# A selective-scan layer in double steps, with a column for the first state ahead of each scan

## The chip, the core and the metric

The kernel runs on one core of one Trainium2 chip. The metric is the device time of one execution in microseconds (us). The engines are TensorE (PE in the profile, PEld for its weight loads), VectorE (DVE), ScalarE (ACT), GpSimd (POOL) and SyncE (SP), which issues the DMAs. SBUF is the on-chip working memory, PSUM the memory that TensorE writes to.

## What is computed

Four layers stand one behind the other on an image batch of 3 x 256 channels x 48 x 48, each as x + layer(groupnorm(x)): a convolution block with attention, a convolution with weights mixed from eight experts, a plain 3x3 convolution, and a selective state space layer (Mamba). Only the last one is touched by the change. It is, for tokens l of one image:

```
xn = layernorm(x)                         # over the 256 channels
x_in, z = in_proj(xn)                     # 512 channels each
u = silu(causal_conv(x_in))               # 4 taps
dt_raw, B, C = x_proj(u)                  # 16 + 16 + 16 values a token
dt = softplus(dt_proj(dt_raw) + bias)
h[d, n] = h[d, n] * exp(dt[d] * A[d, n]) + dt[d] * u[d] * B[n]     # token by token, 16 states n
y[d] = sum over n of h[d, n] * C[n] + u[d] * D[d]
out = out_proj(y * silu(z)),  x = x + out
```

## The kernel before

The layer's code starts at L995. The 2304 tokens of an image are cut into chunks of CH = 384, six an image, 18 in all. The 512 inner channels are four blocks m of 128. For the recurrence the partitions hold 32 channels times 4 states: a block m has four quarters q of 32 channels, and the 16 states are four groups g of four. So one chunk has 4 (m) x 4 (g) = 16 steps of 4 scans (q), and one scan is one VectorE instruction over 128 partitions and 384 tokens.

The main loop (L1348) goes over `steps`, 288 of them. Step s does:

- `fill(s + 1)`: the inputs dt*u*B of the next step's scans, into a tile `hs`. VectorE makes the first two quarters (L1291) from `ps_r`, rows that TensorE has spread over the partitions (`spread_pe`, L1273); GpSimd makes the other two (L1292) from rows that DMAs have spread (`spread`).
- four scans (L1360) in place on `hs`. Each multiplies by a decay exp(dt*A), which ScalarE has written to a PSUM tile `ps_da` (`decay`, L1304), and starts from a state of the chunk before (`state[m, g]`, a per-partition operand), or from 0.0 in the first chunk of an image. The decays come from a pool of three tiles, and behind the scan with running number n the decay n + 3 is issued.
- a ScalarE copy of the last column of the four scans to `state[m, g]` (L1372).
- the product with C on GpSimd (L1375) into a tile `hc`.
- `add_states(s - 2)`: TensorE sums the states of one channel (L1320) into `ps_y`, which also gets u*D (L1316).
- `gate`, two steps into the next block: VectorE multiplies `ps_y` by silu(z) (L1327).

Beside this the loop does the work for the chunks around the present one. `plan`, `after` and `gating` list stages by place: the number j = 4m + g of the step, and where in it (MID: behind the second scan; LATE: behind the fourth; PE_: behind add_states). The stages share one PSUM tile of two banks, `bank` (`ps_g`). Those of interest here: `group_scale` (ScalarE, L1062), `channel_mean` (TensorE, L1069), `centre` (VectorE subtraction L1075, ScalarE square L1077), `inverse_root` (ScalarE, L1081), `normalise` (VectorE, L1086), `tokens` (ScalarE, L1096), `taps` (TensorE, L1105), `take_u` (ScalarE, L1112), `silu` (ScalarE with a table load before and after, L1117), `softplus` (ScalarE, three instructions, L1157), `take_dt` (VectorE twice, L1163, then a ScalarE copy), `project_y` (TensorE, L1188) and `store` (VectorE addition of the residual, L1199, then the DMA out).

`keep_order` (L1397) ties PE, DVE, ACT and POOL to the order in which the source issues. So each of these engines works through its list in that order, and an instruction that waits holds up all that stand behind it on its engine. Which instruction waits for which count of which engine's semaphore is worked out by the tile framework from the tiles that are read and written. SP's list is not tied.

Of the kernel before, what the change touches and what calls it, by code (L numbers as in the profile page):

```python
# [9 lines left out]
F32 = mybir.dt.float32  # L10
I32 = mybir.dt.int32
AF = mybir.ActivationFunctionType
ALU = mybir.AluOpType
AX = mybir.AxisListType
PSUM = bass.MemoryType.PSUM

P = 128
# [3 lines left out]
CT = 2  # L21
# [4 lines left out]
CH = 384  # L26
NCH = N // CH
# [7 lines left out]
DI = 4  # L35
# [47 lines left out]
def net(  # L83
# [20 lines left out]
    nc = tc.nc  # L104
# [13 lines left out]
    def v(name, i=0, n=1):  # L118
# [3 lines left out]
    ident = const.tile([P, P], F32, name="ident")  # L122
# [6 lines left out]
        out=gview, in_=gview, pattern=[[-8, 16], [0, 8]], compare_op=ALU.is_ge,  # L129
# [3 lines left out]
        out=gview, in_=gview, pattern=[[8, 16], [0, 8]], compare_op=ALU.is_ge,  # L133
# [4 lines left out]
    mean2 = const.tile([P, P], F32, name="mean2")  # L138
# [205 lines left out]
    with ExitStack() as l0:  # L344
# [39 lines left out]
        with ExitStack() as p1:  # L384
# [3 lines left out]
            for b in ORDER:  # L388
# [12 lines left out]
                for m in range(2):  # L401
                    for ct in range(CT):
                        nc.tensor.matmul(
                            pb[:, m : m + 1], w("cv1", ct * 256 + m * P, P), sh[:, ct : ct + 1],
                            start=ct == 0, stop=ct == CT - 1,
                        )
                bb = small.tile([P, 2], F32, name="bb")
# [3 lines left out]
                for c in range(NCH):  # L411
                    for m, dst in ((0, y1), (1, cur[b])):
                        pm = ps.tile([P, 512], F32, tag="s", name="ps_y")
                        for ct in range(CT):
                            nc.tensor.matmul(
                                pm[:, :CH], ws[:, ct, m * P : (m + 1) * P], chunk(xb[:, ct, :], c),
                                start=ct == 0, stop=ct == CT - 1,
# [67 lines left out]
        with ExitStack() as p2:  # L485
# [9 lines left out]
            for i in range(NB):  # L495
# [268 lines left out]
                for mt in range(0, NT, 2):  # L764
                    pv = pair()
                    for j in range(2):
                        nc.tensor.matmul(
                            pv[:, j, :384], cur[2][:, (mt + j) * P : (mt + j + 1) * P], wn[2],
                            start=True, stop=True,
# [19 lines left out]
                if i + 1 < NB:  # L789
# [4 lines left out]
                    for b in ORDER:  # L794
                        for c in range(NCH):
                            f = hidden(b, c)
# [69 lines left out]
        chunks = [(b, c) for b in ORDER for c in range(NCH)]  # L866
# [15 lines left out]
        for n, b in enumerate(ORDER):  # L882
            held = None
            for c in range(NCH):
                f = hidden(b, c)
# [31 lines left out]
    with ExitStack() as l1:  # L917
# [55 lines left out]
        for n, (k, h) in enumerate(halves):  # L973
            layer, b = units[k]
# [17 lines left out]

    with ExitStack() as l3:  # L995
        wp = l3.enter_context(tc.tile_pool(name="w3", bufs=1))
        act = l3.enter_context(tc.tile_pool(name="act", bufs=2))
        scn = l3.enter_context(tc.tile_pool(name="scn", bufs=2))
        psd = l3.enter_context(tc.tile_pool(name="psd", bufs=3, space=PSUM))
        psr = l3.enter_context(tc.tile_pool(name="psr", bufs=1, space=PSUM))  # L1000
        psg = l3.enter_context(tc.tile_pool(name="psg", bufs=1, space=PSUM))
        psy = l3.enter_context(tc.tile_pool(name="psy", bufs=1, space=PSUM))
# [32 lines left out]
            )  # L1035
        fold = rep[:, 0, :]

        diag = wp.tile([P, DI, P], F32, name="diag")
        for m in range(DI):
            nc.vector.tensor_scalar(diag[:, m, :], ident, v("D", m), None, ALU.mult)  # L1040
# [3 lines left out]
        def fetch(at):  # L1044
            k = chunks[at] = Chunk()
            k.b, k.c = todo[at]
            k.before = chunks.get(at - 1)
            k.xg = act.tile([P, CT, CH], F32, name="xg")
            nc.sync.dma_start(k.xg, xd[k.b][:, :, k.c * CH : (k.c + 1) * CH])
# [14 lines left out]
                    bias=sh[:, ct : ct + 1], scale=sc[:, ct : ct + 1],  # L1064
                )

        def channel_mean(src, j):
            for ct in range(CT):
                nc.tensor.matmul(  # L1069
                    bank[:, j, :CH], mean2, src[:, ct, :], start=ct == 0, stop=ct == CT - 1  # L1070
                )

        def centre(k):
            mu = bank[:, 0, :CH].unsqueeze(1).broadcast_to([P, CT, CH])
            nc.vector.tensor_tensor(k.xg, k.xg, mu, ALU.subtract)  # L1075
            k.sq = act.tile([P, CT, CH], F32, name="sq", bufs=1)
            nc.scalar.activation(k.sq, k.xg, AF.Square)  # L1077

# [107 lines left out]
        def project_y(k, mo):  # L1186
            for m in range(DI):
                nc.tensor.matmul(  # L1188
                    bank[:, mo, :CH], w("out", m * 256 + mo * P, P), k.sz[:, m, :],
                    start=m == 0, stop=m == DI - 1,  # L1190
                )

        def residual(k):
            k.ot = act.tile([P, CT, CH], F32, name="ot")
            nc.sync.dma_start(k.ot, xd[k.b][:, :, k.c * CH : (k.c + 1) * CH])

        def store(k, mo):
            o = k.ot[:, mo, :]
            nc.vector.tensor_tensor(o, bank[:, mo, :CH], o, ALU.add)  # L1199
            nc.sync.dma_start(  # L1200
                out[k.b, mo * P : (mo + 1) * P, k.c * CH : (k.c + 1) * CH], o
            )

        MID, LATE, PE_ = range(3)
        plan = [
            (12, MID, 2, group_scale),
            (12, PE_, 2, lambda k: channel_mean(k.xg, 0)),
            (13, MID, 2, centre),  # L1210
            (13, PE_, 2, lambda k: channel_mean(k.sq, 1)),
            (14, MID, 2, inverse_root),
            (14, LATE, 2, normalise),
            (15, MID, 2, tokens),
# [22 lines left out]
            (4, MID, -1, residual),  # L1237
            (6, PE_, -1, lambda k: project_y(k, 0)),
            (6, PE_, -1, lambda k: project_y(k, 1)),
            (7, LATE, -1, lambda k: store(k, 0)),  # L1240
            (7, LATE, -1, lambda k: store(k, 1)),
        ]

        gating = [
# [8 lines left out]
        def run(at, j, place):  # L1253
            for when, where, rel, stage in after + plan + gating:
                if (when, where) == (j, place) and 0 <= at + rel < len(todo):
                    stage(chunks[at + rel])

        def spread(k, m):

            dtr = scn.tile([P, 4, CH], F32, name="dtr")  # L1260
            dtur = scn.tile([P, 2, CH], F32, name="dtur")
            for i in range(4):
                r = slice(32 * i, 32 * i + 32)
                nc.sync.dma_start(dtr[r], k.dtd[:, m, :].rearrange("(q d) n -> d q n", d=32))
                nc.sync.dma_start(dtur[r], k.dtud[:, m, :].rearrange("(q d) n -> d q n", d=32))
            return dtr, dtur
# [10 lines left out]
            k.ps = t  # L1277


        steps = [(at, m, g) for at in range(len(todo)) for m in range(DI) for g in range(4)]  # L1280
        chunks = {}
        tiles = {}
        state = {}

        def fill(s):

            at, m, g = steps[s]
            k = chunks[at]
            bb = k.bc[0][:, g, :].unsqueeze(1).broadcast_to([P, 2, CH])
            hs = tiles[s] = scn.tile([P, 4, CH], F32, name="hs", bufs=4)  # L1290
            nc.vector.tensor_tensor(hs[:, 0:2, :], k.ps[:, :, :CH], bb, ALU.mult)  # L1291
            nc.gpsimd.tensor_tensor(hs[:, 2:4, :], k.rows[m][1], bb, ALU.mult)  # L1292

        decays = []

        def decay(n):

            s, q = divmod(n, 4)
            if s >= len(steps):
                return  # L1300
            at, m, g = steps[s]
            da = psd.tile([P, 512], F32, tag="d", name="ps_da")
            col = (m * 4 + g) * 4 + q
            nc.scalar.activation(  # L1304
                da[:, :CH], chunks[at].rows[m][0][:, q, :], AF.Exp, scale=amat[:, col : col + 1]
            )
            decays.append(da)

        def add_states(s):

            at, m, g = steps[s]
            k = chunks[at]
            hc = tiles.pop(s)
            if g == 0:
                k.y_ps = psy.tile([P, 512], F32, name="ps_y")
                nc.tensor.matmul(  # L1316
                    k.y_ps[:, :CH], diag[:, m, :], k.u[:, m, :], start=True, stop=False
                )
            for q in range(4):
                nc.tensor.matmul(  # L1320
                    k.y_ps[32 * q : 32 * q + 32, :CH], fold, hc[:, q, :],
                    start=False, stop=g == 3,
                )

        def gate(at, m):
            k = chunks[at]
            nc.vector.tensor_tensor(k.sz[:, m, :], k.y_ps[:, :CH], k.sz[:, m, :], ALU.mult)  # L1327
# [17 lines left out]
        for _, _, _, stage in gating:  # L1345
            stage(k)

        for s, (at, m, g) in enumerate(steps):  # L1348
            k = chunks[at]
            j = 4 * m + g  # L1350
            if j == 2 and at + 2 <= last:
                fetch(at + 2)
            if s + 1 < len(steps):
                fill(s + 1)

            if g == 2 and s + 2 < len(steps):
                spread_pe(chunks[steps[s + 2][0]], steps[s + 2][1])
            hs = tiles[s]
            for q in range(4):
                nc.vector.tensor_tensor_scan(  # L1360
                    hs[:, q, :], decays[q][:, :CH], hs[:, q, :],
                    0.0 if k.c == 0 else state[m, g][:, q : q + 1], ALU.mult, ALU.add,
                )
                decay(4 * s + q + 3)
                if q == 1:
                    if g == 2 and s >= 6:
                        gate(*steps[s - 6][:2])
                    run(at, j, MID)
            del decays[:4]
            if k.c < NCH - 1:  # L1370
                h = state[m, g] = wp.tile([P, 4], F32, name=f"hst{m}{g}")
                nc.scalar.copy(h.unsqueeze(2), hs[:, :, CH - 1 : CH])  # L1372
            cb = k.bc[1][:, g, :].unsqueeze(1).broadcast_to([P, 4, CH])
            hc = tiles[s] = scn.tile([P, 4, CH], F32, name="hc", bufs=3)
            nc.gpsimd.tensor_tensor(hc, hs, cb, ALU.mult)  # L1375
            run(at, j, LATE)
            if s >= 2:
                add_states(s - 2)
            run(at, j, PE_)
            if g == 1 and m + 1 < DI:  # L1380
                k.rows[m + 1] = spread(k, m + 1)
            elif g == 1 and at < last:
                chunks[at + 1].rows = {0: spread(chunks[at + 1], 0)}
        end = len(steps) - 1
        add_states(end - 1)
        add_states(end)
        gate(*steps[end][:2])
        k = chunks[last]
        residual(k)
        for mo in range(2):  # L1390
            project_y(k, mo)
        for mo in range(2):
            store(k, mo)
        keep_order(tc, listed, mark)


# [110 lines left out]
```

## Time and profile before

| | |
|---|---|
| median of 3 runs | 3840.74 us (3837.43 to 3844.24) |
| the profiled execution | 3840.89 us |
| its span, first to last instruction | 3839.1 us |
| mean granted TensorE clock | 0.901 |
| layers 0 to 2 | 0 to 2165 us |
| last layer up to its first scan | 2165 to 2257.7 us |
| scan loop | 2257.7 to 3819.6 us |
| from the last scan to the end | 3819.6 to 3839.1 us |

| group (one kind of instruction) | engine | count | mean ns |
|---|---|---|---|
| scan with a state operand (L1360) | DVE | 960 | 997 |
| scan from 0.0 (L1360) | DVE | 192 | 937 |
| decay (L1304) | ACT | 1152 | 581 |
| fill, VectorE's half (L1291) | DVE | 288 | 934 |
| fill, GpSimd's half (L1292) | POOL | 288 | 1819 |
| product with C (L1375) | POOL | 288 | 3443 |

In the profile's groups, each row has line, engine, operation, out<-in by tile names, shapes, count, then busy time in us, mean ns of one, and behind the second bar the idle time of the engine just before these instructions, with what ended most of it. "Idle before <- ACT ps_da L1304" means: this engine stood still, and ACT's instruction of line 1304 on tile ps_da released it. TensorE's fp32 matmuls stand in the trace as two records each.

### The profile page before, as it was taken

Reading aid. Unit: us, or ns where it says so; the run is one execution under the profiler, and the core shown is the slowest. Engines: PE = TensorE matmul, PEld = TensorE weight load, DVE = VectorE, ACT = ScalarE, POOL = GpSimd, SP = SyncE. Lnnn points to the kernel's source line nnn. Section 1 sums busy time; section 2 is a strip of 40 time slices with the busy share of each in tenths; the row PEclk is TensorE's granted clock in tenths of the full one; section 3 lists DMA queues with packets and bytes.
Section 4 is the critical chain, followed back from the end, with each engine's and each line's share of the span. In section 5 each row is a group of like instructions: output and inputs, shape, how many; then the busy total and the mean of one; then the engine's idle time right before and its main releaser. Section 6 shows DMA issues by size and latency. Waiting matters only on the chain. (4 is left out here: it accounts for less than half of the span.)

```text
span 3839.1 us, 45642 instructions
## 1 busy us (share of the span) xinstructions
PE 3232.1 (84%) x17010; PEld 1406.6 (37%) x17010; DVE 3221.5 (84%) x3518; ACT 2228.0 (58%) x3216; POOL 1554.8 (40%) x674
## 2 busy tenths in 40 slices
PE   7999999999999988677699757777878878777874
PEld 4323232432323234355577523333333333333331
DVE  4898989779899963799988349999999999999997
ACT  2788787668878762210000147666677666667763
POOL 0000000000000002100000039999999999999998
PEclk9999999999999999888899878888888888888886
DMA  4000000000000015555101133434443433343441
GB/s 170 3 1 1 1 2 1 26 13 1 1 1 2 1 57 173 174 177 177 45 25 42 59 71 100 105 99 104 103 104 91 108 91 99 100 112 92 111 100 34
DMA packets 149962, 266.50 MB, mean 69 GB/s; under 512 B 23441, under 2 KB 123601, under 8 KB 147170
## 3 DMA queue, kind: packets, MB, share of 16 engines
q1 hardware_dynamic: 137634, 245.80, 22.9%
q10 hardware_dynamic: 12096, 17.70, 1.4%
q8 instruction: 135, 2.21, 0.2%
q14 instruction: 97, 0.79, 0.1%
HBM read 216.31 MB, written 46.89 MB: 69 GB/s over the span
## 5 line engine op out<-in xcount | busy, mean ns | idle before, releaser
L587 ACT ACTIVATE pt<-ps_s 128x1024 f32<-128x1024 f32 x972 | 939.0, 1022 | 237.3 <-PE ps_s L583 219.9
L1375 POOL TENSOR_TENSOR hc<-hs,bc 128x1536 f32<-128x1536 f32 x288 | 991.4, 3443 | 85.6 <-DVE hs L1360 56.7
L663 DVE TENSOR_TENSOR part<-part,pt 128x2048 f32<-128x2048 f32 x396 | 906.6, 2289 | 78.4 <-ACT pt L587 53.8
L1360 DVE TENSOR_TENSOR_SCAN hs<-ps_da,hst,hs 128x384 f32<-128x384 f32 x960 | 909.8, 997 | 23.5 <-ACT ps_da L1304 19.9
L1304 ACT ACTIVATE ps_da<-dtr,amat 128x384 f32<-128x384 f32 x1152 | 657.1, 581 | 359.0 <-DVE hs L1360 339.9
L160 POOL TENSOR_TENSOR rstd<-ve,mhalf 128x2 f32<-128x2 f32 (+1 forms) x26 | 17.5, 675 | 1661.7 <-DVE ve L158 1661.7
L583 PE MATMUL ps_s<-q,kt 32*128 32x512 f32 (+1 forms) x4320 | 616.4, 595 | 2.3 <-DVE q L544 0.9
L1292 POOL TENSOR_TENSOR hs<-dtur,bc 128x768 f32<-128x768 f32 x288 | 523.8, 1819 | 77.5 <-DMA dtr<-dtd 77.5
L596 PE MATMUL acc<-pt,vt 128*32 128x512 f32 (+1 forms) x4320 | 523.5, 563 | 8.2 <-DVE o L643 8.0
L927 PE MATMUL ps_c<-vt,u 128*128 128x288 f32 x1728 | 437.8, 417 | 92.9 <-DVE u L257 55.1
L1105 PE MATMUL ps_g<-xn,wtap 128*128 128x384 f32 x1152 | 392.2, 493 | 36.3 <-ACT u L1112 31.3
L927 PEld LDWEIGHTS ps_c<-vt,u 128*128 128x128 f32 x1728 | 335.4, 195 | 190.0 <-issue 56.3
L583 PEld LDWEIGHTS ps_s<-q,kt 32*128 32x128 f32 x4320 | 220.2, 184 | 389.6 <-issue 230.0
L1320 PE MATMUL ps_y<-hc,rep 128*32 128x384 f32 x2304 | 293.5, 596 | 34.6 <-POOL hc L1375 32.7
L1291 DVE TENSOR_TENSOR hs<-ps_r,bc 128x768 f32<-128x768 f32 x288 | 269.1, 934 | 61.8 <-PE ps_r L1273 61.8
L1105 PEld LDWEIGHTS ps_g<-xn,wtap 128*128 128x128 f32 x1152 | 212.7, 189 | 220.1 <-ACT u L1112 54.9
L596 PEld LDWEIGHTS acc<-pt,vt 128*32 128x32 f32 x4320 | 95.7, 108 | 364.3 <-issue 328.5
L943 ACT COPY cb<-ps_c 128x288 f32<-128x288 f32 x48 | 19.0, 395 | 355.5 <-PE ps_c L927 258.5
L1360 DVE TENSOR_TENSOR_SCAN hs<-ps_da,hs 128x384 f32<-128x384 f32 x192 | 170.7, 937 | 17.9 <-ACT ps_da L1304 17.7
L1176 PE MATMUL ps_g<-xn,w3sb 128*128 128x384 f32 x288 | 133.8, 608 | 58.1 <-ACT sz L1184 43.3
L1069 PE MATMUL ps_g<-xg,mean 128*128 128x384 f32 x72 | 52.7, 887 | 105.3 <-ACT dt L1167 78.2
L1320 PEld LDWEIGHTS ps_y<-hc,rep 128*32 128x32 f32 x2304 | 51.3, 118 | 239.1 <-POOL hc L1375 113.5
(204 smaller groups left out, 3265.5 us busy)
## 6 DMA issues: line engine op xcount, KB each, us to landing
wconv<-in_we SPq DMA_DIRECT2D x144, 384.0 KB, 4.3
dtr<-dtd SPq DMA_DIRECT2D x288, 192.0 KB, 3.6
bc<-bcd SPq DMA_DIRECT2D x144, 192.0 KB, 5.9
dtur<-dtud SPq DMA_DIRECT2D x288, 96.0 KB, 2.7
dtd<-dt SPq DMA_DIRECT2D x18, 768.0 KB, 3.5
yc<-ycat ACTq DMA_DIRECT2D x18, 576.0 KB, 5.3
xb<-in_x SPq DMA_DIRECT2D x6, 1152.0 KB, 11.1
ycat<-cur SPq DMA_DIRECT2D x6, 1152.0 KB, 4.9
```

The source lines that it names most:

```text
L583: nc.tensor.matmul(s[:, j, cols], kt[r, mt * P : (mt + 1) * P], q[r, :n], start=True, stop=True,)
L587: nc.scalar.activation(p[:, h0 : h0 + 2, :], s, AF.Exp)
L596: nc.tensor.matmul(acc[h * HD : (h + 1) * HD, :n], vt[:, mt, g * P + h * HD : g * P + (h + 1) * HD], p[:, h, cols], start=mt == 0, stop=mt ...
L663: nc.vector.tensor_tensor(part, first_p if group == 1 else part, p, ALU.add)
L927: nc.tensor.matmul(pc[:, :HN], u[:, i, dy, ct, m * P : (m + 1) * P], vt[:, i, ct, dy * TW : dy * TW + HN], start=ct == 0 and dy == 0, stop ...
L1105: nc.tensor.matmul(bank[:, m % 2, :CH], wtap[:, tap, ct, m * P : (m + 1) * P], k.xn[:, ct, tap : tap + CH], start=tap == 0 and ct == 0, st ...
L1291: nc.vector.tensor_tensor(hs[:, 0:2, :], k.ps[:, :, :CH], bb, ALU.mult)
L1292: nc.gpsimd.tensor_tensor(hs[:, 2:4, :], k.rows[m][1], bb, ALU.mult)
L1304: nc.scalar.activation(da[:, :CH], chunks[at].rows[m][0][:, q, :], AF.Exp, scale=amat[:, col : col + 1])
L1320: nc.tensor.matmul(k.y_ps[32 * q : 32 * q + 32, :CH], fold, hc[:, q, :], start=False, stop=g == 3,)
L1360: nc.vector.tensor_tensor_scan(hs[:, q, :], decays[q][:, :CH], hs[:, q, :], 0.0 if k.c == 0 else state[m, g][:, q : q + 1], ALU.mult, ALU.add,
L1375: nc.gpsimd.tensor_tensor(hc, hs, cb, ALU.mult)
```

## The change

1. A step is now two groups g at once: `steps` runs over (chunk, m, h) with h in 0 and 1, 144 double steps of 8 scans. `fill`, the product with C and the state copies each handle both groups in one instruction per engine. `hs` and `hc` have two buffers each (before: four and three of half the size).
2. Each scan is 385 columns. Column 0 of `hs` holds the first state, copied there by ScalarE (`first_states`, from `state[m, h]` or a tile of zeros), and column 0 of the decay is 0.0, so that the scan starts from the constant 0.0. The decays are three slots of one PSUM tile `slots`, whose first columns are zeroed once; decay n goes to slot n % 3.
3. The fill of the next step is issued behind the eight scans instead of ahead of them, and add_states runs one step late instead of two. `spread` is issued behind the fourth scan of the first half.
4. Layer norm: TensorE makes x - mean at once with matrices `less` (identity minus 1/256, and minus 1/256), four matmuls instead of two; `centre` becomes a ScalarE copy out of PSUM.
5. The residual is added by TensorE with an identity matmul into the accumulation of `project_y`; `store` becomes one ScalarE copy and the DMAs.

```
-        psd = l3.enter_context(tc.tile_pool(name="psd", bufs=3, space=PSUM))
+        psd = l3.enter_context(tc.tile_pool(name="psd", bufs=1, space=PSUM))
...
+        less = wp.tile([P, 2, P], F32, name="less")
+        nc.vector.tensor_tensor(less[:, 0, :], ident, mean2, ALU.subtract)
+        nc.vector.tensor_scalar(less[:, 1, :], mean2, -1.0, None, ALU.mult)
+        zero = wp.tile([P, 8], F32, name="zero")
+        nc.vector.memset(zero, 0.0)
...
+        def less_mean(k):
+            for to in range(CT):
+                for ct in range(CT):
+                    nc.tensor.matmul(
+                        bank[:, to, :CH], less[:, int(to != ct), :], k.xg[:, ct, :],
+                        start=ct == 0, stop=ct == CT - 1,
+                    )
...
         def centre(k):
-            mu = bank[:, 0, :CH].unsqueeze(1).broadcast_to([P, CT, CH])
-            nc.vector.tensor_tensor(k.xg, k.xg, mu, ALU.subtract)
+            nc.scalar.copy(k.xg, bank[:, :, :CH])
...
+            nc.tensor.matmul(bank[:, mo, :CH], ident, k.ot[:, mo, :], start=False, stop=True)
...
+        def store(k):
+            nc.scalar.copy(k.ot, bank[:, :, :CH])
+            for mo in range(CT):
+                nc.sync.dma_start(
+                    out[k.b, mo * P : (mo + 1) * P, k.c * CH : (k.c + 1) * CH], k.ot[:, mo, :]
+                )
...
+        steps = [(at, m, h) for at in range(len(todo)) for m in range(DI) for h in range(2)]
...
+        parts_of_step = [(g, q) for a in range(2) for g in range(2) for q in (2 * a, 2 * a + 1)]
+        slots = psd.tile([P, 3, 512], F32, name="ps_da")
+        nc.vector.memset(slots[:, :, :1], 0.0)
...
+            hs = tiles[s] = scn.tile([P, 2, 4, CH + 1], F32, name="hs")
+            bb = k.bc[0][:, 2 * h : 2 * h + 2, :].unsqueeze(2).broadcast_to([P, 2, 2, CH])
+            nc.vector.tensor_tensor(
+                hs[:, :, 0:2, 1:],
+                k.ps[:, :, :CH].unsqueeze(1).broadcast_to([P, 2, 2, CH]), bb, ALU.mult,
+            )
+            nc.gpsimd.tensor_tensor(
+                hs[:, :, 2:4, 1:],
+                k.rows[m][1].unsqueeze(1).broadcast_to([P, 2, 2, CH]), bb, ALU.mult,
+            )
...
+        def first_states(s):
+            at, m, h = steps[s]
+            src = zero if chunks[at].c == 0 else state[m, h]
+            nc.scalar.copy(tiles[s][:, :, :, 0], src.rearrange("p (g q) -> p g q", g=2))
...
+        def last_states(s):
+            at, m, h = steps[s]
+            if chunks[at].c < NCH - 1:
+                t = state[m, h] = wp.tile([P, 8], F32, name=f"hst{m}{h}")
+                nc.scalar.copy(t.rearrange("p (g q) -> p g q", g=2), tiles[s][:, :, :, CH])
...
-            da = psd.tile([P, 512], F32, tag="d", name="ps_da")
-            col = (m * 4 + g) * 4 + q
             nc.scalar.activation(
-                da[:, :CH], chunks[at].rows[m][0][:, q, :], AF.Exp, scale=amat[:, col : col + 1]
+                slots[:, n % 3, 1 : CH + 1], chunks[at].rows[m][0][:, q, :], AF.Exp,
+                scale=amat[:, col : col + 1],
             )
-            decays.append(da)
...
+        def scan(s, part):
+            g, q = parts_of_step[part]
+            b = tiles[s][:, g, q, :]
+            nc.vector.tensor_tensor_scan(
+                b, slots[:, (8 * s + part) % 3, : CH + 1], b, 0.0, ALU.mult, ALU.add
+            )
...
+        for s, (at, m, h) in enumerate(steps):
...
+            for part in range(8):
+                j = 4 * m + 2 * h + part // 4
+                scan(s, part)
+                decay(8 * s + part + 3)
+                if part % 4 == 1:
+                    if h == 1 and part == 1 and s >= 3:
+                        gate(*steps[s - 3][:2])
+                    run(at, j, MID)
+                if part % 4 == 3:
+                    run(at, j, LATE)
+                if part == 3:
+                    run(at, j, PE_)
...
             if s + 1 < len(steps):
                 fill(s + 1)
-
-            if g == 2 and s + 2 < len(steps):
+                first_states(s + 1)
+
+            if h == 0 and s + 2 < len(steps):
                 spread_pe(chunks[steps[s + 2][0]], steps[s + 2][1])
...
+            last_states(s)
+            times_c(s)
+            if s >= 1:
+                add_states(s - 1)
+            run(at, 4 * m + 2 * h + 1, PE_)
```

## The prediction

> **What bounds the kernel now.** I read the page's engine table first: PE and DVE are both busy 84% of 3839.1 us, which is a mean over layers with different limits and decides nothing. The change touches only the last layer, so I went to the busy times by stage. The scan loop's steady part reads (us; busy time of PE, PEld, DVE, ACT, POOL in this order):
>
> ```profile
> 2340.00:3800.00 1460.00, 1148.78 (x4514) 471.87 (x4512) 1350.18 (x1547) 997.92 (x1788) 1397.77 (x541) 0.85 0.39 99
> ```
>
> POOL is busy 96% of it and DVE 92%. The groups say with what, and for whom they wait:
>
> ```profile
> L1375 POOL TENSOR_TENSOR hc<-hs,bc 128x1536 f32<-128x1536 f32 x288 | 991.4, 3443 | 85.6 <-DVE hs L1360 56.7
> L1360 DVE TENSOR_TENSOR_SCAN hs<-ps_da,hst,hs 128x384 f32<-128x384 f32 x960 | 909.8, 997 | 23.5 <-ACT ps_da L1304 19.9
> L1304 ACT ACTIVATE ps_da<-dtr,amat 128x384 f32<-128x384 f32 x1152 | 657.1, 581 | 359.0 <-DVE hs L1360 339.9
> L1292 POOL TENSOR_TENSOR hs<-dtur,bc 128x768 f32<-128x768 f32 x288 | 523.8, 1819 | 77.5 <-DMA dtr<-dtd 77.5
> L1291 DVE TENSOR_TENSOR hs<-ps_r,bc 128x768 f32<-128x768 f32 x288 | 269.1, 934 | 61.8 <-PE ps_r L1273 61.8
> ```
>
> ACT's decays wait for DVE's scans (340 us), but the scans hardly wait for the decays (20 us): the decays run three ahead. The timelines show the same (start, length, engine; the bracket is the idle time before, with what ended it). First DVE, then ACT beside it, then a place where a scan did wait for its decay:
>
> ```profile
> 2808.67 3.49 DVE L1360 TENSOR_TENSOR_SCAN hs<-ps_da,hs 128x384 f32<-128x384 f32 x4
> 2812.07 0.93 DVE L1291 TENSOR_TENSOR hs<-ps_r,bc 128x768 f32<-128x768 f32 x1
> ```
> ```profile
> 2809.64 0.58 ACT L1304 ACTIVATE ps_da<-dtr,amat 128x384 f32<-128x384 f32 x1 [1.01 <-DVE hs L1360]
> 2810.49 0.59 ACT L1304 ACTIVATE ps_da<-dtr,amat 128x384 f32<-128x384 f32 x1 [0.26 <-DVE hs L1360]
> ```
> ```profile
> 2840.08 0.96 DVE L1360 TENSOR_TENSOR_SCAN hs<-ps_da,hs 128x384 f32<-128x384 f32 x1 [0.19 <-ACT ps_da L1304]
> 2840.95 0.53 DVE L1327 TENSOR_TENSOR sz<-ps_y,sz 128x384 f32<-128x384 f32 x1
> ```
> ```profile
> 2839.48 1.07 ACT L1304 ACTIVATE ps_da<-dtr,amat 128x384 f32<-128x384 f32 x2
> ```
>
> Read from them: scans in a row start every 0.8525 us ((3.49-0.93)/3; each overlaps the next's start). A scan alone takes 0.96, a decay 0.585. The first scan ends at 2808.67+0.93=2809.60 and its decay starts 0.04 later; the first decay of 2839.48 ends at 2840.065 and the waiting scan starts 0.02 later. One handoff each way is thus 0.04 and 0.02. The tile of u projections (L1131) is written once per chunk, first at 2313.21 and last at 3702.44, 16 chunks apart: a chunk of 64 scans takes 86.8 us.
>
> **The wait that decides.** Before, each decay writes a tile of its own out of a pool of three, and scan n waits for decay n. After, there is one PSUM tile `slots` with three slots, whose first columns are zeroed once. The source still issues decay n+3 behind scan n. But the built program, which gives for every instruction the semaphore count it waits for, says: the second scan of a step waits for the count that the decay *behind the first scan* sets, and so on; 1006 of 1152 scans wait for decay n+2, which itself waits for scan n-1. The other scans are the first of each step, which wait for ACT's copy of the first states, and the last ones. So the lookahead of three is gone: scan, decay, scan, decay, each waiting for the other. I take this from the built program, not from the diff, which would let slots be three free buffers.
>
> One link is 0.96 + 0.04 + 0.585 + 0.02 = 1.605 us, where it was 0.8525. What stands queued behind the waiting scan on DVE is everything: fills, gates, dt, normalise; POOL's product and TensorE's sums wait for these.
>
> **Sum for one chunk** (8 double steps of 8 scans):
> - Seven links: 11.24 us. Last scan to fill: 0.88 (2840.08 to 2840.95). The fill doubles: 0.93 + 768 columns at (934-536)/384 = 1.04 ns (768-column fill against the 384-column gate, both out of PSUM) = 1.73. Handoff to the next scan 0.03. Step 13.88, chunk **111.0**. The 385th column adds 1 to 2 ns and the dropped state operand saves 60 ns a scan (997 against 937): both are inside 0.96, which is from a scan without it.
> - ACT's other work used to lie beside scans; now only about 0.97 us of each piece does (the next scan beside it). SiLU with its two table loads takes 4.07 (1.28+1.49+1.29), twice: 2x3.1. Softplus 2.45, once 0.3 late by TensorE: 1.8+1.5. take_dt on DVE, 1.86 (2841.40 to 2843.26) less the 0.65 of the decay beside it, once behind a gate: 1.2+1.95. centre is moved to ACT: copy 0.80 + square 0.81, less 0.97: 0.65. inverse_root, waiting about 1 us for square_mean: 2.1. tokens 0.9, normalise 0.2, gates behind late sums 0.6. Together **16.5** (6 to 9 if TensorE is never late, 22 if it is colder).
> - A chunk: 127.5 against 86.8.
>
> **The other edits.** centre (0.93) and store (2x0.53) leave DVE: 2 us a chunk that would help a DVE-bound loop; in a chain of links DVE's own length matters only where it is in the chain, so I count none, at most 2 us a chunk, 36 us, in both directions. TensorE gets two more matmuls in less_mean and two in project_y, each two records in the trace: 8 records at 0.35 (project_y now) to 0.73 (the first mean after an idle stretch), 3 to 6 us in a chunk whose TensorE work was 1149/16.8=69 us; it has 127 now, so nothing but the lateness priced above. The state copies (0.18 each) stay 16 a chunk; the one ahead of a step lies under the fill (0.96+0.04+0.59+0.18 against 2.61). store's copy (0.80) sits at the same place with 1.0 us of cover. POOL: from 1.78 and 3.40 start to start, 0.165 fixed and 2.10 ns a column, so 3.40 + 6.63 = 10.03 a double step, 80.2 a chunk: hidden under 127. Without that cover it would be the bound (rival A). spread moves forward on SP, past store's DMAs: its rows are needed 14 us and more later, and before nothing in the loop waited for them after the start. The set-up operations are a few at 0.3 us, hidden in the 10 us DVE waits for the first mean.
>
> Whole: first scan at 2257.7, 5 us of start-up stalls as now, 16 chunks of 127.5, one of 125 (the next but one has no LN), one of 114.5 (no next chunk; it keeps one SiLU), less 1.8: last scan ends near 4541. Now 19.5 us follow the last scan; +1.9 (product 6.65 instead of the 4.8 that remained) +1.6 (4 more records) -0.2: 22.8. Span 4563; the profiled run took 3840.89 for 3839.1, so **4565 us**. The median of the runs shown, 3840.74, is the profiled time within 0.2 us, so nothing is corrected.
>
> Bounds: a link with 0.931 and no more than 0.04 handoffs is 1.55 (-55 us over 1006), with 0.99 and 0.12 is 1.69 (+85); extras from 9 to 22 a chunk are -130 to +100. Both ends together are unlikely: 4480 to 4650.
>
> **Rules of the skill.** Before's trace shows decays of one tile running beside the scan of another (2809.64 beside the second scan). The Trainium skill, "PSUM — Partial Sum Buffer", section "PSUM bank collisions raise a hardware error", asks engines to be kept apart by 2 KiB bank and quadrant; the slots are 512 columns of 4 bytes, so by it a decay of one slot could run beside a scan of another; a sum by that rule is rival A's or B's. The built program's waits are stricter than the rule, and they are what runs. Its page "Perfetto Trace Analysis", section "Optimizing Scalar/DVE Operations", says that larger instructions help a saturated engine, but that smaller ones can finish sooner where an engine only makes others wait; by the first half POOL's saving of 2.6 us a chunk would be the result. No run here shows it yet.
>
> **Rivals.**
> - A, POOL sets the pace (2%). If each scan waits only for its own decay, DVE needs 64 scans x 0.855 + 8 fills x 1.65 (start to start) + 8 waits of a scan for its fill x 0.12 + 6.4 (gates 1.8, dt 3.7, normalise 0.9) = 75.3 a chunk and POOL 80.2 is the bound: 17.5 chunks x 6.6 = 115 us less, 3730. For it: POOL is 96% busy now. Against: the waits above. It decides if a decay is done by the time its scan before it ends, that is, if a link is under 0.9.
> - B, no links, but ACT's in-order queue delays the first states (2%). The copy stands behind two decays and, at two places, SiLU and store or softplus: stall 4.07+0.8-1.6 = 3.2, 2.0, 0.9; SiLU ahead of four scans 2.1; gates, less_mean and take_u 4. With 75.3 that is 87.8, 1 us above now: 3860.
> - C, links as forecast, but ACT's pieces hidden wholly (5%): with no extras at all 18x111 and the same ends give 4285; 4285 to 4480.
> - D, links, and TensorE so cold between its bursts that ACT waits for it at every piece (10%): above 4650. For it: 0.73 us a record in the first mean after 4.75 us idle.
>
> The forecast itself has 81%. Faster by over 0.2%, which is about what a measurement here can tell from no change: A, and a little, 0.03. Within 0.2%: 0.01. Slower: 0.96.
>
> **What will show it.** In the changed profile: scans with idle time before nearly each one ended by ACT's decays, some 0.65 us x 1006 = 650 us in that group; decays still waiting for scans; scans 1.6 us apart; POOL busy falling to about 65% of the loop, with the product at 6.6 us; the loop some 725 us longer and layers 0 to 2 unchanged. Wrong would be: scans 0.85 us apart (A or B; then look whether POOL or the first-state copy is last), or a link far from 1.6.

## The result and the profile after

The changed kernel takes **4674.29 us** (median of 4 runs, 4669.71 to 4674.54), the kernel before beside it 3839.09 us (3836.68 to 3844.24): a ratio of 1.2171, with a 95% interval of 1.2149 to 1.2192. The forecast was 4565, with a range up to 4650: the direction and the mechanism are there, and the time is 109 us above the forecast and 24 above the range.

The profiled execution spans 4672.5 us. A part of the loop, in the columns of the stage view shown for the kernel before:

```profile
2400.00:4400.00 2000.00, 1232.56 (x4222) 543.29 (x4215) 1212.60 (x1217) 947.24 (x1668) 1150.48 (x243) 0.77 0.27 66
```

No engine is the bound any more. VectorE, 92% busy before, has 61% (1212.60 of 2000), GpSimd 58% instead of 96%, TensorE's granted clock is 0.77 instead of 0.85. Where every engine idles a quarter of the time or more, waits set the pace, and the groups of the page name them:

```profile
L1346 DVE TENSOR_TENSOR_SCAN hs<-ps_da,hs 128x385 f32<-128x385 f32 x1152 | 1103.1, 958 | 837.8 <-ACT ps_da L1338 805.5
L1338 ACT ACTIVATE ps_da<-dtr,amat 128x384 f32<-128x384 f32 x1152 | 672.6, 584 | 1139.7 <-DVE hs L1346 1125.3
L1354 POOL TENSOR_TENSOR hc<-hs,bc 128x3072 f32<-128x3072 f32 x144 | 886.0, 6153 | 1012.1 <-DVE hs L1346 986.2
...
L1314 POOL TENSOR_TENSOR hs<-dtur,bc 128x1536 f32<-128x1536 f32 x144 | 493.6, 3428 | 89.2 <-DMA dtur<-dtud 78.1
...
L1288 PE MATMUL ps_r<-dtu,rep 32*128 32x384 f32 x288 | 108.1, 835 | 414.9 <-DVE hs L1310 414.9
...
L1310 DVE TENSOR_TENSOR hs<-ps_r,bc 128x1536 f32<-128x1536 f32 x144 | 249.4, 1732 | 0.0
```

Read the first two rows together: scans wait 805.5 us for decays, and decays wait 1125.3 us for scans. Before, only the second of these was there (19.9 us against 339.9). Two engines that wait for each other run in turns. The timeline of VectorE shows it, with the idle time and its releaser in the brackets; the first four rows are the start of an undisturbed step, the last is a scan behind SiLU on ScalarE's list:

```profile
2936.56 0.96 DVE L1346 TENSOR_TENSOR_SCAN hs<-ps_da,hs 128x385 f32<-128x385 f32 x1
2938.17 0.96 DVE L1346 TENSOR_TENSOR_SCAN hs<-ps_da,hs 128x385 f32<-128x385 f32 x1 [0.65 <-ACT ps_da L1338]
2939.78 0.96 DVE L1346 TENSOR_TENSOR_SCAN hs<-ps_da,hs 128x385 f32<-128x385 f32 x1 [0.65 <-ACT ps_da L1338]
2941.39 0.96 DVE L1346 TENSOR_TENSOR_SCAN hs<-ps_da,hs 128x385 f32<-128x385 f32 x1 [0.65 <-ACT ps_da L1338]
...
2958.53 0.96 DVE L1346 TENSOR_TENSOR_SCAN hs<-ps_da,hs 128x385 f32<-128x385 f32 x1 [3.73 <-ACT ps_da L1338]
```

The scans start 1.61 us apart; the forecast link was 1.605. The waits by line in the same 2000 us (total, times, longest) hold something that the forecast had put at 0.6 us a chunk:

```profile
DVE hs L1346 <- ACT ps_da L1338: 682.3, 741, 3.7
DVE sz L1378 <- PE ps_y L1371: 83.0, 57, 1.8
```

The gates (L1378) wait 83 us for TensorE's sums. TensorE's timeline beside one of them (2986.20, a wait of 1.81 us) shows why the sums are late:

```profile
2981.76 1.65 PE L1288 MATMUL ps_r<-dtu,rep 32*128 32x384 f32 x4 [7.22 <-DVE hs L1310]
2983.34 2.79 PE L1371 MATMUL ps_y<-hc,rep 128*32 128x384 f32 x16
```

TensorE stands still for 7.22 us until VectorE's fill has read the old rows, makes the new ones (`spread_pe`), and only then comes to the sums, which end at 2986.13.

### The profile page after: what moved, and what is told of

It reads as the page before. It is cut to its first block, busy times and chain, and to the rows that moved or that the text cites. A ratio compares the mean times of both kernels' runs of the same rounds, so it can differ in the third digit from the quotient of the medians.

```text
span 4672.5 us, 45291 instructions
## 1 busy us (share of the span) xinstructions
PE 3441.2 (74%) x17154; PEld 1533.1 (33%) x17154; DVE 3230.6 (69%) x3324; ACT 2280.0 (49%) x3276; POOL 1441.5 (31%) x386
## 5 line engine op out<-in xcount | busy, mean ns | idle before, releaser
L1346 DVE TENSOR_TENSOR_SCAN hs<-ps_da,hs 128x385 f32<-128x385 f32 x1152 | 1103.1, 958 | 837.8 <-ACT ps_da L1338 805.5
L1338 ACT ACTIVATE ps_da<-dtr,amat 128x384 f32<-128x384 f32 x1152 | 672.6, 584 | 1139.7 <-DVE hs L1346 1125.3
L1354 POOL TENSOR_TENSOR hc<-hs,bc 128x3072 f32<-128x3072 f32 x144 | 886.0, 6153 | 1012.1 <-DVE hs L1346 986.2
L1120 PE MATMUL ps_g<-xn,wtap 128*128 128x384 f32 x1152 | 451.3, 554 | 104.4 <-ACT sz L1199 63.1
L1314 POOL TENSOR_TENSOR hs<-dtur,bc 128x1536 f32<-128x1536 f32 x144 | 493.6, 3428 | 89.2 <-DMA dtur<-dtud 78.1
L1288 PE MATMUL ps_r<-dtu,rep 32*128 32x384 f32 x288 | 108.1, 835 | 414.9 <-DVE hs L1310 414.9
L1120 PEld LDWEIGHTS ps_g<-xn,wtap 128*128 128x128 f32 x1152 | 246.9, 219 | 317.1 <-issue 84.3
L1310 DVE TENSOR_TENSOR hs<-ps_r,bc 128x1536 f32<-128x1536 f32 x144 | 249.4, 1732 | 0.0
L1078 PE MATMUL ps_g<-xg,less 128*128 128x384 f32 x144 | 87.6, 782 | 178.4 <-ACT dt L1182 151.2
L1164 PE MATMUL ps_g<-dbc,dtsb 17*128 17x384 f32 x144 | 102.5, 862 | 115.8 <-ACT dt L1182 62.9
L1288 PEld LDWEIGHTS ps_r<-dtu,rep 32*128 32x128 f32 x288 | 33.6, 278 | 469.0 <-DVE hs L1310 455.7
```

The source lines that it names most:

```text
L1120: nc.tensor.matmul(bank[:, m % 2, :CH], wtap[:, tap, ct, m * P : (m + 1) * P], k.xn[:, ct, tap : tap + CH], start=tap == 0 and ct == 0, st ...
L1310: nc.vector.tensor_tensor(hs[:, :, 0:2, 1:], k.ps[:, :, :CH].unsqueeze(1).broadcast_to([P, 2, 2, CH]), bb, ALU.mult,)
L1314: nc.gpsimd.tensor_tensor(hs[:, :, 2:4, 1:], k.rows[m][1].unsqueeze(1).broadcast_to([P, 2, 2, CH]), bb, ALU.mult,)
L1338: nc.scalar.activation(slots[:, n % 3, 1 : CH + 1], chunks[at].rows[m][0][:, q, :], AF.Exp, scale=amat[:, col : col + 1],)
L1346: nc.vector.tensor_tensor_scan(b, slots[:, (8 * s + part) % 3, : CH + 1], b, 0.0, ALU.mult, ALU.add)
L1354: nc.gpsimd.tensor_tensor(hc, tiles[s][:, :, :, 1:], cb.broadcast_to([P, 2, 4, CH]), ALU.mult)
```

## The experiments

Theories: **L**, the one tile of three slots makes scan and decay alternate. **K**, its rival, the alternation comes from the extra column or from ScalarE and VectorE sharing PSUM, not from the tile. **G**, the gates are late because `spread_pe` stands ahead of the sums on TensorE and waits for VectorE's fill (414.9 us in the page's L1288 row). **H**, its rival, TensorE is just slow after idle time.

### Three tiles instead of one (undo the link)

```diff
-        slots = psd.tile([P, 3, 512], F32, name="ps_da")
-        nc.vector.memset(slots[:, :, :1], 0.0)
+        slots = [psd.tile([P, 512], F32, name=f"ps_da{i}") for i in range(3)]
+        for t in slots:
+            nc.vector.memset(t[:, :1], 0.0)
...
-                slots[:, n % 3, 1 : CH + 1], chunks[at].rows[m][0][:, q, :], AF.Exp,
+                slots[n % 3][:, 1 : CH + 1], chunks[at].rows[m][0][:, q, :], AF.Exp,
```

> The changed kernel with one edit: the three decay slots are three PSUM tiles instead of one. Theory L (link): one tile for three slots makes each scan wait for the decay issued behind the scan before it, 1.61 us a link instead of 0.85. Then scans wait only for their own decay again, the idle time of scans on decays falls from 805 us to under 150, and the time is 3700 to 3900 us: near 3700 if POOL (3.43 + 6.15 us a double step as measured, 77 us a chunk) sets the pace, near 3870 to 3900 if the first-state copies in ACT's queue and late gates do (88 to 90 us a chunk). Rival K: the alternation comes from the extra column or from ACT and DVE sharing PSUM, not from the tile; then the time stays within 2% of 4674.

Measured: 3905.23 us, ratio to before 1.0174 (1.0157 to 1.0191). This is 5 us above the expected range. 769 of the 835 us are gone, with the column and the shared PSUM kept, so L holds and K falls. There are three slots of 512 columns in PSUM as before; only what the framework treats as one tile has changed. The page's scan row, and a stretch of VectorE's timeline:

```profile
L1347 DVE TENSOR_TENSOR_SCAN hs<-ps_da,hs 128x385 f32<-128x385 f32 x1152 | 1006.9, 937 | 226.5 <-ACT hs L1323 179.0
```
```profile
2938.14 1.73 DVE L1311 TENSOR_TENSOR hs<-ps_r,bc 128x1536 f32<-128x1536 f32 x1
2943.27 6.91 DVE L1347 TENSOR_TENSOR_SCAN hs<-ps_da,hs 128x385 f32<-128x385 f32 x8 [3.40 <-ACT hs L1323]
2950.09 1.73 DVE L1311 TENSOR_TENSOR hs<-ps_r,bc 128x1536 f32<-128x1536 f32 x1
2953.23 1.81 DVE L1347 TENSOR_TENSOR_SCAN hs<-ps_da,hs 128x385 f32<-128x385 f32 x2 [1.41 <-ACT hs L1323]
```

Eight scans now run in one piece of 6.91 us. What is left is rival B's picture: the first scan of a step waits for the copy of the first states, which stands late in ScalarE's list. At 2943.27 it waits behind SiLU and `store`: 3.40 us, where rival B had worked out 3.2.

### One tile in the kernel before (the link alone)

```diff
-        psd = l3.enter_context(tc.tile_pool(name="psd", bufs=3, space=PSUM))
+        psd = l3.enter_context(tc.tile_pool(name="psd", bufs=1, space=PSUM))
...
+        slots = psd.tile([P, 3, 512], F32, name="ps_da")
...
-            da = psd.tile([P, 512], F32, tag="d", name="ps_da")
+            da = slots[:, n % 3, :]
```

> The kernel before with one edit: the decays go to three slots of one PSUM tile instead of three tiles of a pool. Theory L: three links of 1.65 us and 1.8 us around the fill make a step of 6.75 us, 107 us a chunk, and 15 to 20 us of ACT's and DVE's other work no longer hidden: 4450 to 4600 us. Rival K: 3840 as before.

Measured: 4478.04 us, ratio 1.166 (1.1641 to 1.168). Three lines, no change of the work, 640 us. The pair of rows that gives it away, from the page:

```profile
L1361 DVE TENSOR_TENSOR_SCAN hs<-ps_da,hst,hs 128x384 f32<-128x384 f32 x960 | 972.8, 1014 | 564.5 <-ACT ps_da L1305 564.5
...
L1305 ACT ACTIVATE ps_da<-dtr,amat 128x384 f32<-128x384 f32 x1152 | 673.0, 584 | 1071.2 <-DVE hs L1361 1054.1
```

So L holds from both sides: taken out of the changed kernel it returns 769 us, put into the kernel before it costs 640.

### The sums ahead of the spread's products (theory G)

```diff
+            if s >= 1:
+                add_states(s - 1)
             if h == 0 and s + 2 < len(steps):
                 spread_pe(chunks[steps[s + 2][0]], steps[s + 2][1])
             last_states(s)
             times_c(s)
-            if s >= 1:
-                add_states(s - 1)
```

> The changed kernel with one edit: on TensorE the sums of states (add_states) stand ahead of spread_pe instead of behind it. In the changed profile three of four gates a chunk wait 1.7 to 1.8 us for these sums. Theory G: they are late because spread_pe ahead of them waits for the fill on DVE; then these waits vanish and 4 to 5 us a chunk go, 4580 to 4610 us. Rival H: TensorE is just slow after idle time (granted clock 0.7); then the gates still wait over 1 us and the time is above 4645.

Measured: 4595.09 us, ratio to before 1.1969 (1.1949 to 1.1989), 79 us less than the changed kernel. G holds: the order alone, with the granted clock no higher (0.75 against 0.77), removes the waits, so H falls. The waits of VectorE in the same 2000 us have no gate in them:

```profile
DVE hs L1346 <- ACT ps_da L1338: 727.7, 810, 5.0
DVE hs L1346 <- POOL hs L1314: 10.8, 15, 0.7
```

The scans' waits are 45 us more in this window, in which more scans fit (810 waits instead of 741).

### The first-state copy on VectorE

The kernel with three tiles, and `nc.scalar.copy` in `first_states` replaced by `nc.vector.tensor_copy`.

> e1 with one more edit: the first states are copied into the column by DVE behind its fill, not by ACT. Theory Q (queue): in e1 scans wait up to 3 us for ACT's copy behind SiLU and softplus, 6 to 9 us a chunk; then this kernel is 60 to 130 us faster than e1, down to POOL's pace of about 77 to 80 us a chunk, 3690 to 3750 us. Rival: POOL already sets the pace in e1 and nothing moves by over 0.5%.

Measured: 4369.22 us, ratio 1.1377 (1.1358 to 1.1396). A miss by over 600 us, for 144 copies of eight columns. The page's row of the 120 copies of a saved state (the other 24 copy zeros):

```profile
L1323 DVE COPY hs<-hst 128x8 f32<-128x8 f32 x120 | 572.3, 4769 | 0.0
```

4.77 us for eight columns, which take ScalarE 0.19 us. The timeline of both engines shows why:

```profile
3004.26 1.73 DVE L1311 TENSOR_TENSOR hs<-ps_r,bc 128x1536 f32<-128x1536 f32 x1
3004.48 6.15 POOL L1357 TENSOR_TENSOR hc<-hs,bc 128x3072 f32<-128x3072 f32 x1 [3.67 <-DVE hs L1349]
3005.90 4.76 DVE L1323 COPY hs<-zero 128x8 f32<-128x8 f32 x1
```

The copy starts while GpSimd's product runs and ends with it: 3005.90+4.76 = 3010.66, 3004.48+6.15 = 3010.63. The fill ahead of it and the scans behind it, which read one operand from PSUM, run beside GpSimd undisturbed. So this run does not tell whether ScalarE's list is what is left; the next pair moves the copy within that list.

### The first-state copy earlier, and the sums first

The kernel with three tiles; `first_states(s + 1)` also allocates the `hs` tile of that step, and stands behind the seventh scan's decay. The second kernel of the pair adds the order of the sums.

```diff
                 decay(8 * s + part + 3)
+                if part == 6 and s + 1 < len(steps):
+                    first_states(s + 1)
...
                 fill(s + 1)
-                first_states(s + 1)
```

> Three separate tiles as in the run with three tiles (3905 us), and the first-state copy of the next step is issued on ScalarE behind the seventh scan's decay of this step, not behind the eighth's decay and the late stage there. Theory Q (without the link, what holds the loop is ScalarE's queue ahead of that copy): in the run with three tiles the scans waited 179 us for the copy, 103 times; that goes, and up to 70 us come back as waits for decays behind the SiLU and softplus pairs and for the gates, so 3730 to 3800 us. Theory P (GpSimd's pace, 6.16+3.44 = 9.6 us a step, 76.8 a chunk): not under 3690. If the copy's lateness was only a mark of something else, 3880 to 3910.

Measured: 3856.92 us, ratio 1.0058 (1.0041 to 1.0075): 48 us less than with three tiles alone, not 105 to 175.

> The kernel with the early first-state copy, and the sums over states ahead of the spread's products on TensorE. In the run with three tiles the gates waited 19 us and the step with inverse_root's wait 15 us in 15 chunks, so the order of the sums is worth 20 to 40 us there if theory G (the gate waits for sums that stand behind the spread's products) holds without the link too: 20 to 40 us below the kernel with the early copy alone, 3700 to 3780. If the gates' lateness is given back by GpSimd's pace, the same time as without it, within 10 us.

Measured: 3816.37 us, ratio 0.9957 (0.994 to 0.9974): 41 us less again, and the only version that is below the kernel before by more than its interval. VectorE's waits from 2400 to 3750 us, first with the early copy alone, then with the sums first too:

```profile
DVE hs L1348 <- ACT hs L1324: 104.6, 77, 2.1
DVE sz L1380 <- PE ps_y L1373: 37.3, 30, 2.6
DVE hs L1348 <- ACT ps_da L1340: 21.5, 20, 1.7
DVE xg L1101 <- ACT sz L1199: 19.8, 15, 1.8
```
```profile
DVE hs L1348 <- ACT hs L1324: 103.5, 77, 2.1
DVE hs L1348 <- ACT ps_da L1340: 42.1, 32, 2.4
DVE xg L1101 <- ACT sz L1199: 6.4, 15, 0.5
```

With three tiles alone the copy was waited for 154.7 us in this stretch; one place earlier makes it 104.6. The order of the sums takes the gates' 37.3 and 13 of `normalise`'s wait, and gives 21 back to the decays. The queue theory is right about where the wait is and wrong about its cure: the copy is late because long pieces (SiLU 4.07, softplus 2.45, or a copy that waits for TensorE's taps) stand ahead of it on ScalarE's list, and one place does not get it past them. In the second kernel a SiLU with its table loads runs from 2983.90 to 2987.98, one decay follows, the copy starts at 2988.52, and the scan behind it has waited 2.11 us.

### The LN edits alone, and taken back

The kernel before with `less_mean`, `square_mean`, the residual by TensorE and the copies on ScalarE:

> The kernel before, with only the LN and residual edits (less_mean, square_mean, the copies on ScalarE). Vector engine loses 0.93 (centre) + 2x0.55 (the two adds) + 0.8 of waits ahead of the adds = 2.8 us a chunk. If the loop before follows VectorE (1252 of 1350 us busy): 3838-17.5x2.8 = 3790. If it follows GpSimd (1290 of 1350 us busy, 60 idle): only what GpSimd waits for scans can go, 3800 to 3838. If ScalarE's added copies delay decays (0.8+0.8 us a chunk behind TensorE): 3840 to 3880. I expect 3800 to 3838.

Measured: 3865.37 us, ratio 1.0083 (1.0066 to 1.01): 30 us slower, the third case of the expectation, though not the one I had named. In the same stretch, scans wait for decays (before, then this kernel):

```profile
DVE hs L1360 <- ACT ps_da L1304: 23.2, 22, 1.9
```
```profile
DVE hs L1371 <- ACT ps_da L1315: 81.0, 72, 1.9
```

VectorE's busy time shrank from 1252 to 1205 us of 1350 (some 20 of that because fewer steps fit, 245 fills instead of 249), and its scans wait 58 us more for decays. That these waits set the time is not shown. GpSimd is the busiest engine in both kernels (1290 and 1266 us). It waits less for scans than before (40.3 us instead of 47.8) and more for a DMA (before, then this kernel):

```profile
POOL hc L1375 <- DMA bc<-bcd: 10.2, 10, 1.1
```
```profile
POOL hc L1386 <- DMA bc<-bcd: 43.5, 16, 3.2
```

That DMA brings the rows of B and C. It follows a ScalarE copy (L1142) that now waits 28.2 us for TensorE's product for x_proj, and this product waits 29.6 us for the copy of `store`, which ScalarE now makes (before, 6.3 for VectorE's additions). Both the decays' and this DMA's lateness come with the edits; no run separates them, so it stays open which of them costs the 30 us.

The same edits, taken back in the fastest kernel:

> The kernel with the early copy and the sums first (3816 us), with the LN and residual edits taken back: the mean and its subtraction, and the two residual adds, are VectorE's again. In the kernel before those edits alone cost 30 us, though VectorE lost work. Theory A (what they add to ScalarE's and TensorE's queues, 0.8+0.8 us of copies and four more matmuls of 0.77 a chunk, delays decays and first-state copies by more than VectorE wins): 15 to 50 us less than 3816, so 3765 to 3800. Theory V (in the double steps VectorE sets the pace, so 0.93+1.1 us of its work and 0.8 of waits a chunk come back): 3816+17x2.5 = 3840 to 3865.

Measured: 3864.84 us, ratio 1.0077 (1.0063 to 1.0091): 48 us slower than with them. Theory A falls here, and theory V's range holds the time, at its upper end. VectorE's waits in this kernel:

```profile
DVE hs L1337 <- ACT hs L1313: 61.0, 47, 2.3
DVE xg L1090 <- ACT sz L1188: 46.3, 15, 3.1
DVE hs L1337 <- ACT ps_da L1329: 31.6, 15, 2.4
DVE ot L1203 <- PE ps_g L1192: 17.0, 15, 1.1
DVE xg L1079 <- PE ps_g L1073: 6.6, 15, 0.4
```

`normalise` (L1090) waits 46.3 us instead of 6.4, the additions and `centre` 23.6 more. Against that, the scans wait 53 us less (61.0 and 31.6 instead of 103.5 and 42.1), so the waits as a whole rise by 13 us only. The rest fits VectorE's own work: `centre` and two additions at 0.95 and 2 x 0.55 us are 31 us in 15 chunks. The same edits thus cost 30 us beside single steps and bring 48 beside double ones: their price depends on the schedule they stand in.

### The column

Three tiles and double steps, each scan starting from the operand of the state, no copy; then the same with the sums first and the LN edits taken back (double steps alone).

```diff
-                b, slots[(8 * s + part) % 3][:, : CH + 1], b, 0.0, ALU.mult, ALU.add
+                b[:, 1:], slots[(8 * s + part) % 3][:, 1 : CH + 1], b[:, 1:], first, ALU.mult, ALU.add
```

> Double steps with three tiles, but without the column: each scan starts from the operand of the state, as in the kernel before (384 columns, first value 0.0 or a column of the saved state), and there is no first-state copy. The scans with an operand take 0.997 us in the kernel before, those without 0.937, so 960 scans cost 58 us more than with the column; the waits for the copy, 179 us in the run with three tiles, go. Theory Q: 3905-179+58 = 3784, and up to 50 more for waits that come back: 3780 to 3835. If the column itself were worth its place: 3905 or more.

Measured: 3867.24 us, ratio 1.0084 (1.0068 to 1.0101). 38 us less than with the column and the late copy, not 70 to 125. Of the waits that went, the gates took 29 back in the stretch (47.9 us for the sums instead of 19.1) and `normalise` 14. Beside the early copy (3856.92) the kernel without the column is 10 us slower.

> Double steps alone: three tiles, scans that start from the operand (no column, no copy), sums first, LN and residual as in the kernel before. Against the kernel without the column (3867 us): the order of the sums gives 40 us as it did beside the early copy, theory A gives 15 to 50 more: 3780 to 3815. Against the kernel with the early copy and LN of before it shows the column alone: by the scans' durations (0.997 with an operand, 0.937 without, 960 of them) 58 us slower, by the first pair (3857 with the column, 3867 without) 10 us slower.

Measured: 3858.8 us, ratio 1.0062 (1.0049 to 1.0076): not 3780 to 3815, since theory A on which that rested had fallen. It is 6 us below its pair with the column (3864.84), and neither 58 nor 10 us above it. With the LN stages of the kernel before, the column is worth nothing: the 0.06 us a scan that it saves, some 51 us in the stretch from 2400 to 3750, stands against 61.0 us of waits for its copy.

## Why the prediction was right, and where it fell short

**The wait that decides: right.** It was read from the built program's waits, not from the diff, and both experiments with the tile confirm it: 1.61 us from scan to scan against 1.605, 3905 us without the link. The Trainium skill, "PSUM — Partial Sum Buffer", section "PSUM bank collisions raise a hardware error", would have engines kept apart by bank; with three tiles of 512 columns decays and scans do run beside each other, at 0.85 us a scan. The waits of the one-tile kernel are the framework's, not the memory's.

**The step: 0.17 us short.** An undisturbed step takes 14.05 us (2936.56 to 2950.61 in the timeline), forecast 13.88. Seven links at 1.61 instead of 1.605 make 0.03. The fifth scan, the first on GpSimd's half of the fill, starts 0.07 later than a link. Another 0.07 lies between the fill and the next scan (1.83 instead of 1.76).

**ScalarE's pieces: right as a sum.** SiLU's scan waits 3.73, which is 3.08 beyond a link's 0.65; forecast 3.1. Softplus waits 2.30 and 1.99, 1.65 and 1.34 beyond; forecast 1.8 and 1.5. `inverse_root` is the one piece that is longer: its scan waits 3.40, 2.75 beyond, forecast 2.1, since ScalarE waits 3.81 for TensorE there and not about 1.

**"Gates behind late sums 0.6": this is the step that failed.** It is mis-sized, and it is not even in the forecast: the terms of the list add up to 17.1 a chunk, and the 16.5 that went into the 127.5 is their sum without the gates' 0.6. I had looked at how long the sums take, not at what stands ahead of them on TensorE. In the changed kernel the gates wait 83.0 us in 2000, 5.5 us a chunk of 133.0 (the chunk read from SiLU of z: first 2288.9, last 4549.4, 17 chunks apart). With the sums first the chunk is 128.7 by the same marks (2286.0 to 4474.1), so the order costs 4.3 a chunk. The remaining 1.3 above the forecast's mean of 127.4 is the step's 0.17 eight times. Eight steps of 14.05 are 112.4, so the extras measure 20.6 a chunk, and 16.3 with the sums first: the other extras together were forecast rightly.

The whole by position in the profiles: the first scan starts at 2269.0 instead of 2257.7 (11.3: the work ahead of it already stands 4.7 later, 2235.05 against 2230.31 for the second part of `take_dt`, and then it waits 6.68 us for its copy, which stands behind `take_z` on ScalarE); from there to the end of the last scan 2377.7 instead of 2282.7 (95.0, of which 76.0 go in the kernel with the sums first, 2301.7; the step's 0.17 in 144 steps would be 24 and more than covers the rest); the end 25.8 instead of 22.8 (3.0). That is 109.3 of the 109.5 by which the span exceeds the forecast. The range's upper end does not follow from its own bounds: extras of 22 a chunk alone were priced at +100, which is 4665. The measured 20.6 lie inside those bounds; with the step, the start and the end on top, all on the same side, the time comes out above 4665 too.

**GpSimd: right in kind.** Product and fill take 6.15+3.43 = 9.58 a step, forecast 10.03. At 76.6 a chunk it was never the bound: 58% busy in the changed kernel (forecast 65), 90% in the fastest kernel (1214.17 of 1350).

**The rivals.** C (pieces of ScalarE hidden) and A (3730) did not come. B named the place and nearly the size of what is left once the link is gone: 3860 worked out (its terms add up to 87.5 a chunk, not 87.8), 3905 measured. It had 6.1 us a chunk for the copy's lateness, and the runs show 154.7 us in 1350, some 10: 90 of 119 first scans of a step wait, six a chunk and not three. D's time came, above 4650, but not by D's mechanism. The cold TensorE is in the trace (clock 0.77, 835 ns a record at L1288), yet ScalarE waits for it at `inverse_root` (57.5 us of 2000) and hardly elsewhere (3.1 at softplus), and changing the order of the sums gave 79 us back at a clock of 0.75. So for that part the queue and not the clock was the cause.

## What to carry to other kernels

Buffers that are meant to be written ahead should be separate tiles: when slots of one tile are cycled by hand, look in the trace for two engines that each wait for the other; here that pair cost 640 to 770 us. When a step is made larger, the in-order lists around it become longer between two useful points, so price each wait by what stands *ahead* of the releaser on its engine, not by how long the releaser takes. And a shift of work between engines has no price of its own: try it again when the schedule has changed, since the same edit can change sign.

## What the runs showed of the hardware that I had not expected

A VectorE copy from SBUF to SBUF of 128x8 values took 4.77 us when GpSimd's product was running and ended within 0.03 us of the product's end. At 2263.77 us of the same run, with GpSimd idle, it took 0.17 us. A fill of 1536 columns with one input from PSUM took 1.73 us beside the product. So in this run the length of the stall is the rest of GpSimd's instruction; no other size of copy was run. The Trainium skill gives a reason: in "SBUF — State Buffer", section "Who interferes with whom", VectorE and GpSimd share a pair of ports that one of them can hold for a whole instruction, and copies are among the operations that can need it. The run agrees, 4.77 us against 0.17.

An in-place scan that takes its first state from a column instead of a per-partition operand takes 0.937 us for 385 columns, against 0.997 for 384 with the operand: the operand costs 0.06 us. The column costs nothing that can be seen: scans of 384 columns from 0.0 take 0.937 as well.
